# Values of later head groups by seven block products, with their exchange and the reciprocals issued from SP's queue

## The chip, the cores and the metric

The kernel runs on one core of one Trainium2 chip. The metric is the device time of one execution in microseconds (us). TensorE is called PE here and its weight loads PEld; VectorE is DVE, ScalarE is ACT, GpSimd is POOL, and SyncE is SP, which in this kernel does nothing but issue DMAs.

## The reference

The input x has 2048 rows of 256 numbers. It is normalised by row (xn), and the output is x plus two branches of xn, everything in float32:

```python
qkv = jnp.einsum('bsd,ed->bse', x, Wqkv)            # x is xn here; 16 heads of 128
logits = jnp.einsum('bqhd,bkhd->bhqk', q, k) * D ** (-0.5)
w = jax.nn.softmax(logits)
out = jnp.einsum('bhqk,bkhd->bqhd', w, v).reshape(B, S, H * D)
return jnp.einsum('bse,de->bsd', out, Wout)
...
x = x + _L0_attn_ref(xn, Wqkv, Wout) + _L0_ffn_ref(xn, w1, w2, w3)
```

The second branch is a small gated layer with weights rounded to -1, 0 and 1; it is done ahead of the attention loop and is not touched here.

## The kernel before, in words

**Blocks and steps.** The transposed xn lies in SBUF as `xnT` (two slices d of 128 by 2048 columns). The attention is cut into 64 blocks n = 0..63: 16 heads times four query blocks of 512. A block has four steps t = 0..3 of 128 queries. Two heads make a group g (G = 2), so a group has eight blocks, and i = n mod 8 says which of them it is. In the text "step (5,3)" means i = 5, t = 3 in any group.

**What one step of the loop at L965 does.** The scores run ahead by LEAD = 6 steps: step u = 4n + t computes the scores of step v = u + 6, exchanges them, transposes the exponentials of step v - 2, and multiplies block n's transposed exponentials with the values. In the order of the program, each engine taking its own instructions in that order:

- `left` of the step before (L1065): DVE adds up the product of values (`added`, L744, at t = 3 with the multiplication by the spread reciprocals in oT, L754) and reads the second projection product, if there was one.
- POOL's differences (`differences`, L662, line L677): the product with the values is done with seven block products in the place of eight, and the exponentials' side of it needs four differences in each block.
- `scores` (L559): PE makes two halves of 1024 keys in PSUM tiles `s`, of which there are three. DVE takes each half's maximum (L579) and the negated maximum (L582). Then `beside` (L990) makes the step's first projection product on PE into the only buffer of tag `m`, and DVE reads it. ACT makes the exponentials (L589); that frees the `s` tile.
- `inverses` (L615) at t = 2: DVE sums and inverts the row sums, transposes them (L627), and POOL sends them to DRAM (`rd`, L628).
- `transposed` (L652): DVE turns two parts of 128x1024 into a slot of R (L657).
- `weighted` (L706): PE multiplies with the values, 16 pairs of matmuls (8 pairs at t = 3), line L724.
- the step's second projection product, into the same `m` buffer, if the step has two; ACT's `copied` (L733).
- `exchanged` (L595): ten DMAs from SP's queue and two from ACT's, 64 KB each, move 32-row pieces of p into two tiles `part0` and `part1` (two buffers each); ACT copies the other four pieces.
- `between` (L929): POOL's DMAs for the output projection, weight loads and small sums.

At t = 1 `spread` (L630) lets POOL read the reciprocals back, broadcast to all partitions, into oT.

**Projection products.** Steps with t = 2, 3 make the keys and queries of the next head (`fast_product`, L163, `fast_read`, L180): seven 128x128x512 products over two blocks in the place of eight. That form pairs two column blocks of xn and leaves one of its two results with its elements in another order, which the read puts right in its output pattern. Steps with t = 0, 1 of blocks i = 0..3 make the output projection of the group before, also by seven products (`o_product`, L803). Steps with t = 0, 1 of blocks i = 4..7 make the values of the next group (`v_product`, L272, `v_read`, L282): eight products, one in each step, each of 16 PE instructions of 256 columns, and two DVE copies of 128x256. These eight steps have no second product. The table `x_sums` (L155) holds differences of xn's column blocks, made once by POOL.

**The order of the work** is written out by hand (`manual_schedule`); tiles of one tag share buffers, and an instruction waits where a buffer or an operand isn't ready.

Of the kernel before, what the change touches and what calls it, by code (L numbers as in the profile page):

```python
# [9 lines left out]
F32 = mybir.dt.float32  # L10
F32R = mybir.dt.float32r
AF = mybir.ActivationFunctionType
ALU = mybir.AluOpType
# [7 lines left out]
def layernorm_attention_bitffn_kernel(  # L21
# [123 lines left out]
    def weight_sums(h: int):  # L145
# [6 lines left out]
        nc.gpsimd.tensor_tensor(w[:, 3], wk[:, 1], w[:, 1], sub)  # L152
        ws[h] = w

    def x_sums(c: int):  # L155
        t = apool.tile([P, 4, QB], F32, tag=f"t{c}", name=f"t{c}", bufs=1)
        x00, x10 = (xnT[:, d, bass.ts(c, QB)] for d in range(KC))
        x01, x11 = (xnT[:, d, bass.ts(c + 1, QB)] for d in range(KC))
        for i, (a, b) in enumerate(((x01, x00), (x11, t[:, 0]), (x11, x01), (x10, t[:, 1]))):
            nc.gpsimd.tensor_tensor(t[:, i], a, b, ALU.subtract)  # L160
        ts[c] = t

    def fast_product(h: int, b: int, i: int, second: bool):  # L163

        c = b // 2 * 2
        wk, wq = (weights[h // G, i][:, :, bass.ts(h % G, D)] for i in "kq")
        w, t = ws[h], ts[c]
        x00, x10 = (xnT[:, d, bass.ts(c, QB)] for d in range(KC))
        x11 = xnT[:, 1, bass.ts(c + 1, QB)]
        lhs, rhs = {  # L170
            (0, 0): ((wk[:, 0], x00), (w[:, 1], t[:, 1])),
            (0, 1): ((w[:, 2], t[:, 2]), (wq[:, 1], t[:, 3])),
            (1, 0): ((w[:, 0], t[:, 0]), (w[:, 3], x11)),
            (1, 1): ((wk[:, 1], x10),),
        }[b % 2, i][second]
        pm = ps_m.tile([P, QB], F32, tag="m", name=f"pw{h}_{b}_{i}_{int(second)}")
        in_halves(pm, lhs, rhs, True, True)
        return pm

    def fast_read(h: int, b: int, i: int, second: bool, pm):  # L180
        c = b // 2 * 2
        if (b % 2, i) == (0, 0):
            if not second:
                if c == 0:
                    kTs[h] = kvpool.tile([P, S], F32, tag="kT", name=f"kT{h}")
                for j in range(2):
                    qTs[h, c + j] = kvpool.tile(
                        [P, QB], F32, tag="qT", name=f"qT{h}_{c + j}", bufs=NB + 2
                    )
        k0, k1 = (  # L190
            kTs[h].rearrange("p (j k r) -> p k j r", j=P // 32, r=32)[:, j * TB : (j + 1) * TB]
            for j in (c, c + 1)
        )
        q0, q1 = qTs[h, c], qTs[h, c + 1]
        pk = pm.rearrange("p (k j r) -> p k j r", j=P // 32, r=32)
        def q_sum(q, base):
            nc.vector.tensor_tensor(q, pm, base, ALU.add)

        def k_sum(k, base):
            nc.vector.tensor_tensor(k, pk, base, ALU.add)  # L200

        if (b % 2, i) == (0, 0):
            if not second:
                nc.vector.tensor_copy(k0, pk)
            else:
                k_sum(k1, k0)
        elif (b % 2, i) == (0, 1):
            if not second:
                nc.vector.tensor_tensor(
                    q1.rearrange("p (k j r) -> p k j r", j=P // 32, r=32), pk, k1, ALU.add  # L210
                )
            else:
                q_sum(q0, q1)
        elif (b % 2, i) == (1, 0):
            if not second:
                q_sum(q1, q1)
            k_sum(k1, k1)
        else:
            k_sum(k0, k0)
# [38 lines left out]

    wxs = {}

    def sums_of(k, q, name: str):

# [4 lines left out]
        nc.gpsimd.tensor_tensor(w[:, 3], k[:, 1], w[:, 1], ALU.subtract)  # L269
        wxs[name] = w  # L270

    def v_product(g: int, m: int, second: bool):  # L272
        w = weights[g, "v"]
        pm = ps_m.tile([P, 2, G * D], F32, tag="m", name=f"pvw{g}_{m}")
        for j in range(2):
            for d in range(KC):
                in_halves(
                    pm[:, j], xnT[:, d, bass.ts(2 * m + j, P)], w[:, d], d == 0, d == KC - 1
                )
        return pm  # L280

    def v_read(g: int, m: int, second: bool, pm):  # L282
        for j in range(G):
            nc.vector.tensor_copy(
                v_tile(g * G + j)[:, 2 * m : 2 * m + 2], pm[:, :, bass.ts(j, D)]
            )

    ppool = ctx.enter_context(tc.tile_pool(name="ppool", bufs=2))
    front = ExitStack()
# [7 lines left out]
    ods = [  # L297
        [away.tile([P, G, QB], F32, tag=f"od{g}_{c}", name=f"od{g}_{c}") for c in range(NB)]
        for g in range(2)
    ]  # L300
    rds = [away.tile([P, 32], F32, tag=f"rd{i}", name=f"rd{i}") for i in range(2)]

# [312 lines left out]
    def inverses(n: int):  # L615
        if n >= NBK - NB:

            r = small.tile([P, TB], F32, tag="rlast", name=f"rlast{n}")
            nc.vector.tensor_tensor(r, sums[n][:, :, 0], sums[n][:, :, 1], ALU.add)
            nc.vector.reciprocal(r, r)  # L620
            rbs[n] = r
            return
        ri, riT = rinvs[n % 2]
        nc.vector.tensor_reduce(ri[:, :TB], sums[n], AX.X, ALU.add)
        nc.vector.reciprocal(ri[:, :TB], ri[:, :TB])

        nc.vector.transpose(riT, ri)  # L627
        nc.gpsimd.dma_start(rds[n % 2], riT)  # L628

    def spread(n: int):  # L630

        if n < NBK - NB:
            r = rds[n % 2].rearrange("(j c) r -> j (c r)", c=32)[:, : TB * 32]
            nc.gpsimd.dma_start(
                oT.rearrange("p (j x) -> p j x", j=P // 32), r.partition_broadcast(P)
            )
            rbs[n] = oT
# [291 lines left out]
    def between(n: int, t: int):  # L929

        g, i = divmod(n, GB)
        last = NBK - NB

        if t == 1:
            if i == GB - 1 and n < last:
                load_weights(g, "o", nc.gpsimd)
        if t == 2:
            if i == NB - 1 and g + 1 < H // G:
                load_weights(g + 1, "v", nc.gpsimd)
            elif n == last - 1:  # L940
                load_weights(g, "o", nc.gpsimd)
        if g and i < NB:
            o_moved(g - 1, i, t)
        elif n < last:
            if i == GB - 2:
                if t < 3:
                    o_fetched(g, *((0, 0, 0), (1, 0, 1), (1, 1, 2))[t])
                else:
                    o_difference(1, 1, 0)
                    o_difference(2, 2, 1)  # L950
            elif (i, t) == (GB - 1, 2):
                y_moved(0, False)
        if n < last and (i, t) == (GB - 1, 3):
            o_sums(g)
        if n >= last - 1 and t == 2:
            b = n + 1 - last
            nc.gpsimd.dma_start(o3[:, b % 2], ods[(H - 2) // G % 2][b][:, 0])
        if (n, t) in ((last - 2, 3), (last - 1, 0)):
            fetched_back(n + 2 - last)
        if t == 0 and n in (last - 3, last - 2, last, last + 1):  # L960
            x_fetched((last - 3, last - 2, last, last + 1).index(n))

    behind = []
    with tc.manual_schedule():
        for u in range(-LEAD, (NBK - 1) * TB):  # L965
# [13 lines left out]
            if n >= NB and t < 2:  # L979
                i, j = divmod(i, NB)  # L980
                j = 2 * j + t
                if not i:
                    seven, hi = True, (g - 1, j)
                    product, read, twice = o_product, o_read, j % NB != 1
                elif g + 1 < H // G:
                    seven, hi = True, (g + 1, j)
                    product, read, twice = v_product, v_read, False
            pms = []

            def beside():  # L990
# [7 lines left out]

            if behind:
                behind.pop()()  # L1000
            if t == 0 and n >= 0:
                if 0 < n <= NBK - NB:
                    put_away(n - 1)
                differences(n, "T1b")
            elif t == 1 and n >= 0:
                differences(n, "T2h")
                if n >= NB and n % GB < NB and n % 2 == 0 and n < NBK - NB:
                    o_difference(0, 2, 0)
                differences(n, "T3b")
                spread(n)  # L1010
                if blocks[n][1] == 0:
                    v_combined(blocks[n][0], 2)
                    v_combined(blocks[n][0], 3)
                differences(n, "T4")
            elif t == 3 and -1 <= n < NBK - 2:
                differences(n + 1, "T1a")
                if n % 2 and n % GB < NB <= n < NBK - NB - 2:
                    y_moved(n % GB, True)
                differences(n + 1, "T3a")
                if n >= 0 and blocks[n + 1][1] == 0:  # L1020
                    v_combined(blocks[n + 1][0], 0)
                    v_combined(blocks[n + 1][0], 1)
# [118 lines left out]
```

## Time and profile before

| what | us |
| --- | --- |
| median of three runs (lowest, highest) | 2160.19 (2158.59, 2161.88) |
| the profiled execution's own time | 2159.7 |
| its span in the trace | 2157.9 |
| PE busy | 2143.5 |
| DVE busy | 1756.1 |
| POOL busy | 1579.3 |
| ACT busy | 1375.1 |
| values of later groups on PE (`pvw`, 896 instructions) | 107.6 |
| their copies on DVE (L284, 112 instructions) | 42.0 |
| POOL idle ahead of the reciprocals' DMA (L628) | 154.2 |
| SP's queue waiting for DVE's transposes (L611) | 206.1 |

The profile is one execution. Busy time is the union of an engine's instructions. The granted clock of PE is full in every slice. The timeline merges equal instructions that follow one another into one row (start, length, line, operation, tiles, shape, number); a row's length is to the end of its last instruction, and consecutive PE instructions overlap, so the pace is read from start to start of two rows. In the rows of the DMA view, the last number is the median time from the start of an issue to the landing.

### The profile page before, as it was taken

What the parts mean: (1) busy time and instruction counts of PE and PEld (TensorE: products, weight loads), DVE (VectorE), ACT (ScalarE), POOL (GpSimd) and SP (SyncE); (2) the same over time, 40 slices, a digit from 0 to 9 for tenths busy, and PEclk for the clock granted to TensorE, in tenths of its full rate; (3) what the DMA queues carried; (4) which work ended last, traced back from release to release, by engine and by line L of the source; (5) the groups of instructions that cost most, each with busy time, mean ns of one, the idle gap of its engine ahead of it and who ended that gap; (6) DMA issues with size and microseconds to landing.
All of it is one profiled execution on the core that took longest, in us unless ns stands there. A gap on an engine that the chain in (4) does not pass through costs nothing. (4 is left out here: it accounts for less than half of the span.)

```text
span 2157.9 us, 41390 instructions
## 1 busy us (share of the span) xinstructions
PE 2143.5 (99%) x14018; PEld 1207.6 (56%) x14018; DVE 1756.1 (81%) x2394; ACT 1375.1 (64%) x2414; POOL 1579.3 (73%) x1010
## 2 busy tenths in 40 slices
PE   9999999999999999999999999999999999999999
PEld 6745445445655555555555455655555555555556
DVE  6577887888888887888788888788888888788885
ACT  5587766666666666666666666666666666666773
POOL 0067767987678867887768876788767887788873
PEclk9999999999999999999999999999999999999999
DMA  2055555575556655566555754556555665556663
GB/s 94 39 119 139 132 117 136 148 187 142 121 140 160 166 141 128 136 184 157 123 128 142 189 151 110 140 145 180 149 122 135 157 173 143 127 138 184 174 151 95
DMA packets 182341, 304.34 MB, mean 141 GB/s; under 512 B 55088, under 2 KB 60592, under 8 KB 182128
## 3 DMA queue, kind: packets, MB, share of 16 engines
q1 hardware_dynamic: 127856, 175.21, 31.9%
q0 software_dynamic: 28720, 91.97, 17.5%
q10 hardware_dynamic: 25552, 34.51, 6.2%
q8 instruction: 111, 1.82, 0.4%
q14 instruction: 102, 0.84, 0.1%
HBM read 65.60 MB, written 34.54 MB: 46 GB/s over the span
## 5 line engine op out<-in xcount | busy, mean ns | idle before, releaser
L677 POOL TENSOR_TENSOR R<-R 128x1024 f32<-128x1024 f32 x441 | 1175.5, 2673 | 144.4 <-DVE R L657 84.7
L94 PE MATMUL s<-kT,qT 128*64 128x512 f32 x4000 | 907.4, 592 | 1.0 <-ACT p L589 0.8
L613 ACT COPY part<-p 32x512 f32<-32x512 f32 x1024 | 630.7, 616 | 417.7 <-issue 306.5
L579 DVE TENSOR_REDUCE mx<-s 128x1 f32<-128x1024 f32 x512 | 618.2, 1220 | 230.5 <-PE s L94 216.7
L589 ACT ACTIVATE p<-s,nm 128x1024 f32<-128x1024 f32 x512 | 565.9, 1110 | 207.8 <-PE pw L94 101.6
L657 DVE STREAM_TRANSPOSE R<-part 128x1024 f32<-128x1024 f32 x512 | 605.1, 1220 | 34.1 <-DMA part<-p 24.4
L94 PEld LDWEIGHTS s<-kT,qT 128*64 128x64 f32 x4000 | 331.7, 137 | 476.2 <-issue 431.8
L724 PE MATMUL av<-R,v 128*64 128x256 f32 x3728 | 531.2, 379 | 1.5 <-DVE oU L750 1.3
L724 PE MATMUL av<-R,st 128*64 128x256 f32 x3024 | 457.7, 379 | 2.5 <-ACT oU L742 1.3
L724 PEld LDWEIGHTS av<-R,v 128*64 128x64 f32 x3728 | 357.7, 137 | 109.7 <-issue 43.9
L724 PEld LDWEIGHTS av<-R,st 128*64 128x64 f32 x3024 | 305.5, 137 | 143.0 <-issue 50.6
L628 POOL DMA_DIRECT2D rd<-r x60 | 33.4, 556 | 154.2 <-DVE r L627 153.9
L742 ACT COPY oU<-av 64x256 f32<-64x256 f32 x248 | 90.7, 366 | 84.5 <-PE av L724 77.0
L780 POOL DMA_DIRECT2D od<-oU x60 | 34.0, 567 | 125.0 <-DVE oU L754 125.0
L750 DVE TENSOR_TENSOR oU<-av,oU 64x256 f32<-64x256 f32 x248 | 101.8, 411 | 27.4 <-ACT oU L742 24.7
L94 PE MATMUL pvw<-wv,xnT 128*64 128x256 f32 x896 | 107.6, 379 | 0.0
L94 PEld LDWEIGHTS pvw<-wv,xnT 128*64 128x64 f32 x896 | 74.8, 137 | 45.7 <-issue 24.2
L589 ACT ACTIVATION_READ_ACCUMULATOR p<-s,nm 128x1 f32 x512 | 100.3, 196 | 0.0
L824 DVE TENSOR_TENSOR osums<-pow,osums 128x512 f32<-128x512 f32 x108 | 72.5, 682 | 29.3 <-DMA osums<-yd 18.3
L94 PE MATMUL pw<-t,ws 128*64 128x512 f32 x336 | 88.4, 592 | 0.0
L160 POOL TENSOR_TENSOR t<-xnT 128x512 f32<-128x512 f32 x4 | 5.1, 1271 | 107.1 <-DMA part<-p 107.1
L200 DVE TENSOR_TENSOR kT<-pw,kT 128x512 f32<-128x512 f32 x112 | 76.8, 686 | 1.8
(153 smaller groups left out, 1484.4 us busy)
## 6 DMA issues: line engine op xcount, KB each, us to landing
part<-p SPq DMA_DIRECT2D x2560, 64.0 KB, 2.3
part<-p ACTq DMA_DIRECT2D x512, 64.0 KB, 2.6
o<-od POOLq DMA_DIRECT2D x74, 256.0 KB, 3.9
oT<-rd POOLq DMA_DIRECT2D x60, 256.0 KB, 5.5
od<-oU POOLq DMA_DIRECT2D x60, 256.0 KB, 2.7
osums<-yd POOLq DMA_DIRECT2D x28, 512.0 KB, 4.8
yd<-osums POOLq DMA_DIRECT2D x26, 512.0 KB, 3.5
yd<-yT SPq DMA_DIRECT2D x4, 512.0 KB, 2.6
```

The lines of the kernel that those rows point to most:

```text
L94: nc.tensor.matmul(out[c * HP : (c + 1) * HP], lhs[:, c * HP : (c + 1) * HP], rhs, start=start, stop=stop, skip_group_check=True,)
L200: nc.vector.tensor_tensor(k, pk, base, ALU.add)
L579: nc.vector.tensor_reduce(mx[:, i : i + 1], s, AX.X, ALU.max)
L589: nc.scalar.activation(p, s, AF.Exp, bias=nm, scale=SCALE, accum_out=sums[n][:, t, i : i + 1],)
L613: nc.scalar.copy(*ends(j, j))
L657: nc.vector.transpose(to[:, t % 2, 2 * i : 2 * i + 2], part.rearrange("p g (s c) -> p g s c", s=2),)
L677: nc.gpsimd.tensor_tensor(o, x, y, ALU.subtract)
L724: nc.tensor.matmul(av[i * HP : (i + 1) * HP, half], l[:, kk], moving(s, kk), start=start, stop=(k == units[r] - 1), skip_group_check=True,)
L742: nc.scalar.copy(u[op, oq], av[ap, half])
L750: nc.vector.tensor_tensor(u[p, q], av[p, half], u[p, q], ALU.add)
L780: nc.gpsimd.dma_start(ods[h // G % 2][b][:, h % G], oU)
L824: nc.vector.tensor_tensor(to, pm, y, ALU.add)
```

## The change

1. The values of groups 1 to 7 are made by seven block products for each half of the 2048 rows (`fast_v_product`, `fast_v_read`), with the two heads of the group in the places that queries and keys have in `fast_product`. So a group has 14 products of 512 columns in its eight steps: two in each of six steps and one in two. DVE reads them with eight operations on 128x512 for each half.
2. The result is the transposed one (128 numbers of a head by rows of x), while the product with the exponentials wants rows of x on partitions. For each head and half, `v_sent` moves four pieces of 32 partitions to DRAM (4 KB in each partition, 1 KB at a time), `v_landed` reads the half back with its pieces exchanged (512 KB, into columns of `xnT` that are no longer needed), and DVE transposes 32x32 blocks with two instructions of 128x512 (`v_transposed`). The table `v_steps` names the step in which each is issued, at the step's beginning in the new function `ahead`.
3. To free those columns of `xnT`, the second pair of column blocks is taken in the opposite order (`pair`).
4. The DMA of the reciprocals to DRAM (`sent_away`) moves from POOL's queue at t = 2 to SP's at the beginning of t = 3, and `spread` from POOL's queue at t = 1 to SP's at the beginning of t = 2.
5. POOL makes four sums of the value weights (`v_sums`) once in each group at (3,3).

```diff
+    def pair(c: int):
+        return (c, c + 1) if c == 0 else (c + 1, c)
...
+    def v_sums(g: int):
+        wv = weights[g, "v"]
+        sums_of(wv[:, :, D:], wv[:, :, :D], f"wvs{g}")
...
-    def v_product(g: int, m: int, second: bool):
-        w = weights[g, "v"]
-        pm = ps_m.tile([P, 2, G * D], F32, tag="m", name=f"pvw{g}_{m}")
-        for j in range(2):
-            for d in range(KC):
-                in_halves(
-                    pm[:, j], xnT[:, d, bass.ts(2 * m + j, P)], w[:, d], d == 0, d == KC - 1
-                )
+    def fast_v_product(g: int, m: int, second: bool):
+        half, m = divmod(m, NB)
+        wv, w, t = weights[g, "v"], wxs[f"wvs{g}"], ts[2 * half]
+        c0, c1 = pair(2 * half)
+        x00, x10 = (xnT[:, d, bass.ts(c0, QB)] for d in range(KC))
+        x11 = xnT[:, 1, bass.ts(c1, QB)]
+        lhs, rhs = (
+            ((wv[:, 0, D:], x00), (w[:, 1], t[:, 1])),
+            ((w[:, 2], t[:, 2]), (wv[:, 1, :D], t[:, 3])),
+            ((w[:, 0], t[:, 0]), (w[:, 3], x11)),
+            ((wv[:, 1, D:], x10),),
+        )[m][second]
+        pm = ps_m.tile([P, QB], F32, tag="m", name=f"pvw{g}_{half}_{m}_{int(second)}")
+        in_halves(pm, lhs, rhs, True, True)
         return pm
...
-            nc.vector.tensor_copy(
-                v_tile(g * G + j)[:, 2 * m : 2 * m + 2], pm[:, :, bass.ts(j, D)]
-            )
...
+        if (m, second) == (0, False):
+            nc.vector.tensor_copy(k0, pm)
+            return
+        todo = {
+            (0, True): ((k1, k0),), (1, False): ((q1, k1),), (1, True): ((q0, q1),),
+            (2, False): ((q1, q1), (k1, k1)), (2, True): ((k1, k1),), (3, False): ((k0, k0),),
+        }[m, second]
+        for o, i in todo:
+            nc.vector.tensor_tensor(o, pm, i, ALU.add)
+
+    def v_sent(h: int, half: int):
+
+        v = v_half(h, half).rearrange("p k d -> p (k d)")
+        vd = vds[h % G][half].rearrange("(j r) (q c) -> q r j c", r=32, c=S // 8)
+        for q in range(P // 32):
+            nc.sync.dma_start(vd[q], v[bass.ts(q, 32)].rearrange("r (j c) -> r j c", c=S // 8))
+
+    def v_landed(h: int, half: int):
+        nc.sync.dma_start(landing, vds[h % G][half])
+
+    def v_transposed(h: int, half: int):
+        v = v_half(h, half).rearrange("p k (q r) -> p q k r", r=32)
+        w = landing.rearrange("p (q k r) -> p q k r", q=P // 32, r=32)
+        for u in range(2):
+            nc.vector.transpose(v[:, 2 * u : 2 * u + 2], w[:, 2 * u : 2 * u + 2])
+
+    wxs, landing = {}, xnT[:, 0, QB : 3 * QB]
...
-        nc.gpsimd.dma_start(rds[n % 2], riT)
+
+    def sent_away(n: int):
+        nc.sync.dma_start(rds[n % 2], rinvs[n % 2][1])
...
-            nc.gpsimd.dma_start(
+            nc.sync.dma_start(
                 oT.rearrange("p (j x) -> p j x", j=P // 32), r.partition_broadcast(P)
             )
...
+        if t == 3:
+            if i == NB - 1 and g + 1 < H // G:
+                v_sums(g + 1)
...
+    v_steps = {
+        (5, 1): [(v_sent, 0, 0)], (5, 2): [(v_landed, 0, 0), (v_sent, 1, 0)],
+        (5, 3): [(v_transposed, 0, 0)], (6, 0): [(v_landed, 1, 0)], (6, 1): [(v_transposed, 1, 0)],
+        (7, 1): [(v_sent, 0, 1)], (7, 2): [(v_landed, 0, 1), (v_sent, 1, 1)],
+        (7, 3): [(v_transposed, 0, 1)], (8, 0): [(v_landed, 1, 1)], (8, 1): [(v_transposed, 1, 1)],
+    }
+
+    def ahead(n: int, t: int):
+
+        if t == 3 and n + 1 < NBK - NB:
+            sent_away(n + 1)
+        if t == 2 and n >= 0:
+            spread(n)
+        g, i = divmod(n, GB)
+        for late in range(2):
+            if late < g + 1 < H // G + late:
+                for do, j, half in v_steps.get((i + late * GB, t), ()):
+                    do((g + 1 - late) * G + j, half)
...
-                    product, read, twice = v_product, v_read, False
+                    product, read, twice = fast_v_product, fast_v_read, j % NB != NB - 1
...
             if behind:
                 behind.pop()()
+            if n >= -1:
+                ahead(n, t)
...
-                spread(n)
```

## The prediction

> **What bounds the kernel now.** I read the page's busy table first, then PE's timeline through a group's last value block (i = 7) into the next block, then DVE, ACT and SP over the same stretch, then the DMA table.
>
> ```profile
> PE 2143.5 (99%) x14018; PEld 1207.6 (56%) x14018; DVE 1756.1 (81%) x2394; ACT 1375.1 (64%) x2414; POOL 1579.3 (73%) x1010
> ```
> ```profile
> 612.63 1.93 PE L94 MATMUL pvw<-wv,xnT 128*64 128x256 f32 x16
> 614.36 3.65 PE L724 MATMUL av<-R,v 128*64 128x256 f32 x32
> 617.81 3.63 PE L94 MATMUL s<-kT,qT 128*64 128x512 f32 x16
> ...
> 635.03 3.63 PE L94 MATMUL s<-kT,qT 128*64 128x512 f32 x16
> 638.46 1.06 PE L94 MATMUL pw<-xnT,wk 128*64 128x512 f32 x4
> 639.32 1.93 PE L724 MATMUL av<-R,v 128*64 128x256 f32 x16
> 641.04 3.63 PE L94 MATMUL s<-kT,qT 128*64 128x512 f32 x16
> ```
>
> PE has no idle time in the loop: every row starts where the last one's issue ended. From start to start: scores 3.43 us, a value product 1.73, a product of 512 columns 0.86, the product with the exponentials 3.45 (1.72 at t = 3). So work taken from PE is time won, as long as no other engine makes PE wait. The nearest is DVE:
>
> ```profile
> 633.28 2.37 DVE L657 STREAM_TRANSPOSE R<-part 128x1024 f32<-128x1024 f32 x2
> 635.58 0.82 DVE L750 TENSOR_TENSOR oU<-av,oU 64x256 f32<-64x256 f32 x2
> 636.43 0.69 DVE L200 TENSOR_TENSOR kT<-pw,kT 128x512 f32<-128x512 f32 x1
> 637.04 1.21 DVE L579 TENSOR_REDUCE mx<-s 128x1 f32<-128x1024 f32 x1
> 638.70 1.23 DVE L579 TENSOR_REDUCE mx<-s 128x1 f32<-128x1024 f32 x1 [0.45 <-PE s L94]
> 639.96 0.21 DVE L582 TENSOR_SCALAR nm<-mx 128x1 f32<-128x1 f32 x1
> ```
>
> This is step (7,3), the shortest of a block (6.0 us of PE): DVE goes from transposes to sums to the first maximum without a pause and has only 0.45 us left ahead of the second. SP is nearly as full: ten exchange DMAs a step at 0.63 us from start to start are 6.3 us of a step of 6.0 to 8.6.
>
> ```profile
> part<-p SPq DMA_DIRECT2D x2560, 64.0 KB, 2.3
> o<-od POOLq DMA_DIRECT2D x74, 256.0 KB, 3.9
> oT<-rd POOLq DMA_DIRECT2D x60, 256.0 KB, 5.5
> osums<-yd POOLq DMA_DIRECT2D x28, 512.0 KB, 4.8
> yd<-osums POOLq DMA_DIRECT2D x26, 512.0 KB, 3.5
> yd<-yT SPq DMA_DIRECT2D x4, 512.0 KB, 2.6
> ```
>
> **Part 1, PE's gain.** A group's values cost 8 x 1.73 = 13.8 us now and 14 x 0.86 = 12.0 after (the new products have the form of the 512-column rows). 1.8 us in seven groups is **-12.6 us**.
>
> **Part 2, DVE's added work, covered or not.** Reads: sixteen operations of 0.68 us (row L200) in the place of sixteen copies of 0.42: +4.2 us a group. Transposes: eight of 128x512; from 0.21 us at 32 columns and 1.22 at 1024, I take 0.70, so 1.3 us for a pair. Summing a block's steps with these rows, blocks 5 and 7 reach about 29.2 us of DVE in 31.0 of PE, blocks 4 and 6 27 to 28 in 32.7. It fits, so by busy time alone this costs nothing; POOL's four sums (2.2 us a group) lie in its idle time too. But the transposes stand in DVE's order ahead of the step's maxima, so what counts is when the data lands.
>
> **Part 3, the landing at (5,3) and (7,3).** No row shows this DMA: 512 KB from DRAM issued by SP. Bounds: 2.6 us (the same size written from SP, on a quiet chip) and 4.8 (the same read issued by POOL, beside the exchange). I take 3.9, the write's 2.6 plus the 1.3 by which POOL's read exceeds its write. The first landing of a half is issued right behind the oT broadcast, which moves to SP too; as a read of the same size from the same queue takes 3.9 and the broadcast 5.5, its small pieces hold the DMA engines 1.6 us longer. Issued 0.6 us ahead, I charge 1.1 us: **5.0** for this one (bounds 2.6 and 4.8 + 1.6 = 6.4).
>
> Now the order on SP. The landing follows the ten exchange DMAs of step (5,1). In the trace the matching ones start with ACT's exponential:
>
> ```profile
> 623.04 1.11 ACT L589 ACTIVATE p<-s,nm 128x1024 f32<-128x1024 f32 x1 [1.16 <-issue]
> ```
> ```profile
> 631.62 0.59 SPq L611 DMA_DIRECT2D part<-p  x1
> ```
>
> Those two rows say that SP ends the ten 9.2 us after the exponential of (7,1) began. Call that E. Then oT's issue, 0.6; landing at E + 9.2 + 0.6 + 5.0 = E + 14.8. DVE gets to the transposes when its sums of (7,2) are done: the exponential of (7,2) comes one PE step later, E + 7.7 (0.9 sooner than now, since step (7,1) loses 1.73 and gains 0.86), and the sums end at 637.04, 5.4 after that step's exponential at 631.65: E + 13.1. **DVE waits about 1.7 us.**
>
> What PE feels: the exponential at 640.25 begins 1.8 us after the scores' issue end at 638.46. It moves by the pair of transposes 1.3 and the wait 1.7, less the slack 0.45: to 4.35. PE wants that first `s` buffer for the second half of the next scores, 0.86 + 1.72 + 1.72 = 4.3 us after 638.46, and it is free 1.15 after the exponential begins, so anything past 3.15 stalls PE. **1.2 us of stall** (the wait less 0.5), twice in a group: 14 x 1.2 = **+16.8 us**. Without the wait the transposes alone fit, with 0.5 us to spare.
>
> **Part 4, the landing at (6,0).** SP issues it behind the exchange of the late (5,3), which ends 8.1 us after its exponential (640.25 to 648.39): 4.35 + 8.1 + 3.9 = 16.35 us after the scores of (5,3). DVE, with step (6,0)'s work done, is there at about 14.8. It waits 1.5, turns (1.3), and the maxima, the negation and the first read (2.4 + 0.1 + 0.6) end at 20.7. PE wants the only `m` buffer for its second product at (6,1) about 20.1 after. Before, value steps had no second product, so this wait is new: **0.6 us**, in seven groups **+4 us**. At (8,1) there is no second product, and the `s` buffers are free in time: nothing.
>
> **Part 5, the rest.** POOL loses 60 issues of rd (0.56) and of oT (0.78) and 154 us of waiting, but PE waits 3.3 us for POOL's differences in all: at most 3 us won, which I don't count. On SP blocks 5 and 7 get eleven more issues, 51 x 0.63 = 32 us of 31.0; the exchange falls behind by 1 to 2 us there, and its pieces land 5 to 7 us ahead of their transposes. So nothing, unless the lag passes 5 us. The reciprocals get a step more and are not needed until (n,3)'s end. 7 x 4 MB of added traffic is 9% of 304 MB.
>
> **Sum.** -12.6 + 16.8 + 4 = +8 us. The profiled execution's own time is 2159.7 (2157.9 of span and 1.8 around it), 0.5 below the median of 2160.2, so I predict **2168**.
>
> **The Trainium skill.** The page "DMA: Bandwidth & Descriptors", section "Anatomy of one DMA", gives 2.0 us plus bytes at 436 GB/s, an estimate of 3.2 us for 512 KB; for 64 KB that is 2.15, beside 2.3 measured here. By it alone both landings are nearly in time, and the sum would be about -11 us. The same page, "Queues, rings and completion order", says that an engine takes the descriptors of one issuer's ring in order. That speaks against moving oT to SP just ahead of a landing; with it the sum stays near the one above. No row of this trace shows that order for oT.
>
> **Rivals.** (A) *The landing is quick*: 3.5 us or less, oT not in its way. For: a 512 KB write from SP takes 2.6. Against: every read in the table is slower than its write. The waits then cost 0 to 6 us: 2148 to 2154. It decides where the first landing takes less than about 3.8 us. (B) *Gain and waits cancel*: at 4.3 to 4.9 us for the first, 2156 to 2164. (C) *oT blocks longer, or the exchange delays it too*: first landing at 6.4 and second at 4.8 gives waits of 3.1 and 2.4, stalls of 2.6 x 14 + 1.5 x 7 = 47, less 12.6: 2195. (D) *SP overflows*: if the exchange lags over 5 us in blocks 5 and 7, DVE's R transposes wait; each further us costs 14. Against: SP itself now waits 206 us for DVE, which it could spend on issues. (E) *PE doesn't take the products at 0.86*: excluded by four rows of that form.
>
> **Chances.** The forecast (first landing 4.9 to 6) 0.35, A 0.30, B 0.22, C and D together 0.13. What a measurement can tell from no change is 0.2%, 4.3 us. Faster: A, 0.31 with a little of B; same: most of B, 0.22; slower 0.47. The range reaches down to A's full gain less a little, 2149, and up into C, 2190; cases of both signs hold it, and the forecast's own range is 2163 to 2182.
>
> **What would show it.** After: `pvw` rows of four instructions at 0.86; on DVE, a wait of 1 to 2 us for the DMA that writes xnT at (5,3) and (7,3), and at (6,1); on PE, scores waiting for ACT's exponentials at (6,0) and (8,0), 1 to 1.5 us each. If DVE shows no such wait, A holds. If DVE's R transposes wait for part, it is D. I am wrong altogether if PE's idle time in the loop stays near zero, or sits in steps that I have not named.

## The result

| kernel | median, us (lowest to highest) | span of the profiled execution | PE idle after 200 us | lost to a lower clock from 200 us to the last stall |
| --- | --- | --- | --- | --- |
| before | 2160.19 (2157.74 to 2161.88) | 2157.9 | 4.8 | 0.0 |
| changed | 2339.93 (2334.5 to 2347.56) | 2343.9 | 140.4 | 66.6 |

The changed kernel is slower: the ratio is 1.0839, with a 95% interval of 1.0814 to 1.0864. The forecast of 2168 and its range to 2190 are missed by 172 and 150 us. The last column is worked out from the granted clock: the length of each stretch at less than full clock times the missing share. Windows at the start and the very end, which no stall of the loop brings, are left out.

### The profile page after: what moved, and what is told of

It reads as the page before. It is cut to its first block, busy times and chain, and to the rows that moved or that the text cites. A ratio compares the mean times of both kernels' runs of the same rounds, so it can differ in the third digit from the quotient of the medians.

```text
span 2343.9 us, 40558 instructions
## 1 busy us (share of the span) xinstructions
PE 2192.1 (94%) x13514; PEld 1058.9 (45%) x13514; DVE 1816.6 (78%) x2450; ACT 1375.6 (59%) x2414; POOL 1513.4 (65%) x918
## 5 line engine op out<-in xcount | busy, mean ns | idle before, releaser
L94 PE MATMUL s<-kT,qT 128*64 128x512 f32 x4000 | 948.8, 615 | 102.2 <-ACT p L645 102.2
L715 DVE STREAM_TRANSPOSE R<-part 128x1024 f32<-128x1024 f32 x512 | 605.2, 1220 | 40.9 <-DMA part<-p 39.6
L94 PEld LDWEIGHTS s<-kT,qT 128*64 128x64 f32 x4000 | 300.1, 141 | 661.7 <-issue 497.5
L782 PEld LDWEIGHTS av<-R,v 128*64 128x64 f32 x3728 | 330.3, 138 | 153.4 <-issue 63.9
L782 PEld LDWEIGHTS av<-R,st 128*64 128x64 f32 x3024 | 287.4, 137 | 196.3 <-issue 74.0
L335 DVE STREAM_TRANSPOSE v<-xnT 128x512 f32<-128x512 f32 x56 | 36.5, 690 | 181.3 <-DMA xnT<-vd 91.5
L849 POOL TENSOR_TENSOR o<-o 128x512 f32<-128x512 f32 x56 | 73.1, 1306 | 1.3
L319 DVE TENSOR_TENSOR v<-pvw,v 128x512 f32<-128x512 f32 x98 | 65.1, 676 | 5.2 <-PE pvw L94 4.9
```

The costliest lines, as they stand in the source:

```text
L94: nc.tensor.matmul(out[c * HP : (c + 1) * HP], lhs[:, c * HP : (c + 1) * HP], rhs, start=start, stop=stop, skip_group_check=True,)
L715: nc.vector.transpose(to[:, t % 2, 2 * i : 2 * i + 2], part.rearrange("p g (s c) -> p g s c", s=2),)
L782: nc.tensor.matmul(av[i * HP : (i + 1) * HP, half], l[:, kk], moving(s, kk), start=start, stop=(k == units[r] - 1), skip_group_check=True,)
L849: nc.gpsimd.tensor_tensor(o3[:, slot], o3[:, x], o3[:, y], ALU.subtract)
```

## The profile after

The page of the changed kernel: the span, the busy table, a group of PE (busy time, mean ns | idle time ahead of it and what ended it), the group of the new transposes, and DMAs that the change adds or moves.

```profile
span 2343.9 us, 40558 instructions
...
PE 2192.1 (94%) x13514; PEld 1058.9 (45%) x13514; DVE 1816.6 (78%) x2450; ACT 1375.6 (59%) x2414; POOL 1513.4 (65%) x918
...
L94 PE MATMUL s<-kT,qT 128*64 128x512 f32 x4000 | 948.8, 615 | 102.2 <-ACT p L645 102.2
...
L335 DVE STREAM_TRANSPOSE v<-xnT 128x512 f32<-128x512 f32 x56 | 36.5, 690 | 181.3 <-DMA xnT<-vd 91.5
...
oT<-rd SPq DMA_DIRECT2D x60, 256.0 KB, 5.6
vd<-v SPq DMA_DIRECT2D x112, 128.0 KB, 2.2
xnT<-vd SPq DMA_DIRECT2D x28, 512.0 KB, 6.5
```

PE has 504 matmuls fewer, and yet its busy time has grown by 49 us and it stands idle. DVE spends 36.5 us on the new transposes and 181.3 us in front of them. So the time is lost where the prediction looked for it, but in another size. The list of waits (us in total, times, longest) has the same places, and that of SP's queue one more, its sends of the values:

```profile
DVE R L715 <- DMA part<-p: 39.6, 30, 3.7
...
PE pvw L94 <- DVE v L319: 31.7, 7, 5.9
```
```profile
SPq L326 <- DMA part<-p: 79.8, 17, 7.9
```

One pass through steps (7,2) to (8,0), on SP, DVE and PE in the timeline (start, length):

```profile
952.84 7.39 SPq L667 DMA_DIRECT2D part<-p  x10
960.39 1.61 SPq L692 DMA_DIRECT2D oT<-rd  x1
962.10 0.45 SPq L329 DMA_DIRECT2D xnT<-vd  x1
967.31 2.29 SPq L326 DMA_DIRECT2D vd<-v  x4
969.71 8.17 SPq L667 DMA_DIRECT2D part<-p  x10
```
```profile
962.58 0.69 DVE L205 TENSOR_TENSOR kT<-pw,kT 128x512 f32<-128x512 f32 x1
968.70 1.30 DVE L335 STREAM_TRANSPOSE v<-xnT 128x512 f32<-128x512 f32 x2 [5.43 <-issue]
...
992.38 1.30 DVE L335 STREAM_TRANSPOSE v<-xnT 128x512 f32<-128x512 f32 x2 [9.00 <-DMA xnT<-vd]
```
```profile
967.22 1.88 PE L94 MATMUL s<-kT,qT 128*64 128x512 f32 x8
973.84 3.63 PE L94 MATMUL s<-kT,qT 128*64 128x512 f32 x8 [4.74 <-ACT p L645]
```

The landing is issued at 962.10, behind oT, and lands at 968.62. DVE, ready at 963.27, waits 5.43 us; the scores' second half then waits 4.74 us for an `s` buffer. The eight matmuls that follow take 3.41 us from start to start of the next row, twice what eight took before (3.43 us for sixteen). The view by windows says why; its columns are the window, its length, PE's busy time, the granted clock, the DMA share and GB/s:

```profile
969.10:973.84 4.74, 0.00 (x1) 1.00 0.59 137
973.84:977.25 3.41, 3.41 (x9) 0.51 0.41 96
977.25:981.61 4.36, 4.36 (x38) 0.99 0.49 139
```

After the stall PE is granted half its clock for a window. In the loop after the first 200 us the trace has 27 such windows of 3.41 or 6.83 us, 133 us together; the kernel before has none there. They are why PE's busy time grew.

Where the time went, by steps: for each step the time from its first scores matmul to the next step's is added up over the groups, and that of the kernel before is taken off (us; the other kernels are the experiments below).

| kernel | (5,1), (7,1) | (6,0) | (6,1), (6,2) | (8,0) | (8,2) | (6,3), (8,1), (8,3) | others | all |
| --- | --- | --- | --- | --- | --- | --- | --- | --- |
| changed | -12.2 | +48.5 | +46.8 | +54.0 | +39.8 | -0.3 | +6.7 | +183.3 |
| reciprocals on POOL | -12.2 | +23.1 | +49.3 | +37.8 | +43.2 | -0.3 | -1.6 | +139.3 |
| transposes five times, no exchange | -12.2 | +45.2 | +16.1 | +41.1 | +9.0 | -0.3 | +15.8 | +114.7 |
| exchange without transposes | -12.2 | +2.1 | +28.7 | +7.1 | 0.0 | +32.5 | +39.5 | +97.7 |
| the same, reciprocals on POOL | -12.2 | -0.1 | +1.3 | +3.8 | 0.0 | +36.5 | +4.4 | +33.7 |
| early landings, POOL sends and lands | -12.2 | -0.1 | -0.1 | 0.0 | 0.0 | +4.4 | -1.6 | -9.6 |

Three things are to be seen. The gain is there in every kernel, in (5,1) and (7,1), the two steps that make one product of 0.86 us in the place of one of 1.73. In the changed kernel the loss sits in four places of seven groups, each of which has one stall; one of the 28 stalls, at (8,2), has no window behind it. And where nothing waits for a landing, the loss is in other steps.

## The experiments

The theories were these. **Landing**: the transposes stand on DVE ahead of the maxima and wait for a landing that comes late, and PE pays for DVE's wait (Parts 3 and 4). **SP**: the values' and the reciprocals' transfers ahead of the exponentials make the exponentials late (rival D). The expectations also name a DVE theory (DVE's added work is too much by itself), and call the SP theory, from run 5 on, that of the queues. Ratios are to the kernel before, run on the same chip, with 95% intervals. Runs 5 to 8 were made on one chip and the others on another; the medians of the kernel before are 1 to 3 us apart, and differences between runs of the two chips carry that much.

**1. The products alone.** The table of the exchange is empty; the reciprocals stay on SP.

```diff
-    v_steps = {
...
+    v_steps = {}
```

> The change without the exchange of the values: seven block products and their reads stay, nothing is sent to DRAM, read back or transposed, so the values of groups 1 to 7 stay in the wrong layout. Landing theory (DVE stands at its transposes until the DMA from DRAM lands, PE stalls behind it 28 times for some 4.9 us and runs at half clock for a while after each): all of the loss goes and PE's gain of 12.6 us shows, 2146 to 2150. DVE theory (the added reads are too much for DVE in blocks 5 and 7): part of the loss stays, above 2200. SP theory (the queue is too full with 140 more issues and the reciprocals): most of the loss goes, but the reciprocals on SP keep some of it, 2165 to 2200.

Measured 2157.66 us, ratio 0.9996 (0.9985 to 1.0007). The steps (5,1) and (7,1) gain 12.2 us; the time doesn't, as PE stands idle 13.0 us, mostly in (2,0) to (4,2), in front of DVE's sums. None of the three expected ranges holds it. Run 15 shows that this comes from the reciprocals.

**2. The transposes without transfers.** The entries of `v_sent` and `v_landed` are taken out of the table.

> As the one before, with DVE's 56 transposes back in their places, but of whatever lies in xnT: no DMA to DRAM or from it, so the transposes wait for nothing. The values of groups 1 to 7 are wrong. Landing theory: the work alone fits, within 4 us of the kernel without them, 2146 to 2152. DVE theory: the transposes' place ahead of the maxima is enough to stall PE, at least 14 times 2 us with half clock after, 2200 or more. SP theory: as the kernel without them.

Measured 2158.97 us, ratio 1.0001 (0.9991 to 1.001), as the run before it. DVE's added work costs nothing by itself; Part 2 stands.

**3. The exchange without the transposes.** The entries of `v_transposed` are taken out.

> The change without DVE's 56 transposes: the pieces are sent to DRAM and read back by SP as in the change, but nobody waits for the landing. The values of groups 1 to 7 are wrong. Landing theory: SP's lag and the traffic cost little, as nobody stands behind them: 2146 to 2160. SP theory: the loss is all there, above 2250, since the exchange of the exponentials comes late by as much as in the change.

Measured 2263.23 us, ratio 1.0488 (1.0459 to 1.0518). Nothing waits for a landing here, and 105 us are lost against run 1. DVE's transposes of the exponentials wait instead, and SP for its earlier transfers:

```profile
DVE R L715 <- DMA part<-p: 173.8, 102, 6.2
```
```profile
SPq L667 <- DMA part<-p: 181.7, 126, 4.6
```

The first was 24.4 us before. So the landing theory alone falls: rival D is real. In the changed kernel it hardly shows (39.6 us); my reading, which no run tests, is that DVE is held at the values' transposes first and SP catches up meanwhile.

**4. The kernel before with the reciprocals on SP.**

```diff
-        nc.gpsimd.dma_start(rds[n % 2], riT)
...
+            if t == 3 and -1 <= n and n + 1 < NBK - NB:
+                sent_away(n + 1)
+            if t == 2 and n >= 0:
+                spread(n)
```

> The kernel before with the reciprocals' two DMAs moved to SP's queue as in the change, and nothing else. Landing theory: not on any path that PE waits for, 2156 to 2164, no difference. SP theory: 120 more issues, one of them of many small pieces in the ring of the exchange, cost something by themselves, 2170 to 2220.

Measured 2171.2 us, ratio 1.0046 (1.003 to 1.0061): 12.3 us for moving two transfers a block, without any values.

**5. The changed kernel with the reciprocals on POOL.** `rd` and oT go back to POOL's queue, to their old places.

> The changed kernel with the two transfers of the reciprocals issued from POOL again, in their old places; the values' products, exchange and transposes as changed. Landing theory (the transposes stand on DVE ahead of their landings, which take 7.1 us in the median behind oT and 5.15 us without it): only the first landing gets shorter, by about 2 us, 14 of 28 stalls shrink by 2 us, and the time is about 2300 us, with DVE still waiting 4 to 7 us at every transpose. Theory of the queues (oT's pieces of 512 bytes hold SP's and ACT's transfers for about 4 us, and the transfers of the exponentials behind them come late): most of the stalls fall under the 2.5 us from which the clock was halved, and the time is between 2160 and 2210 us, with few halved windows. If the time stays within 10 us of 2340 us, the reciprocals have no part in the loss.

Measured 2297.79 us, ratio 1.0652 (1.0629 to 1.0674). DVE's mean wait for the first landing falls from 5.82 to 3.65 us, that for the second only from 7.13 to 6.78. This is what the landing theory expected; 42 of the 180 us belong to the reciprocals.

**6. Run 3 with the reciprocals on POOL.**

> The run with the exchange of the values but without its transposes (2263.2 us), now with the reciprocals issued from POOL; the transposes are left out, so v isn't the reference's. Nothing on an engine waits here for the landings of the values. Theory of the queues with oT as the cause: what is left of the loss goes with oT, 2150 to 2165 us. Theory of the queues with the values' own ten issues per head as the cause (4 to 6 issues of 0.63 us and a landing ahead of the ten of the exponentials): still 2210 to 2250 us, with DVE waiting for part at the same steps as before. Landing theory has nothing to say here, beyond what the transposes would add.

Measured 2189.4 us, ratio 1.0131 (1.0104 to 1.0157), between the two expectations: the reciprocals made 74 us of run 3's loss, the values' own transfers on SP the other 43 (against run 15). DVE still waits 126.9 us for exponentials.

**7. Early landings.** The reciprocals on POOL; the sends of a half's first head and both landings are issued at the end of the step before, just ahead of `exchanged` (the expectations call a step a part). The transposes stay where they were.

```diff
+    v_early = {
+        (5, 0): [(v_sent, 0, 0)], (5, 1): [(v_landed, 0, 0)], (5, 3): [(v_landed, 1, 0)],
+        (7, 0): [(v_sent, 0, 1)], (7, 1): [(v_landed, 0, 1)], (7, 3): [(v_landed, 1, 1)],
+    }
...
+            if n >= 0:
+                v_issued(v_early, n, t)
             if more:
                 exchanged(v)
```

> Reciprocals on POOL, and the landings issued a step part earlier than they were, ahead of that part's ten transfers of the exponentials, so that a landing has a whole part (about 15 us) before its transposes. Landing theory: no transpose waits, no stall is left, and the time is 2146 to 2156 us, which beats the kernel before by 0.2 to 0.6%. Theory of the queues with the values' own issues as the cause: the exponentials' transfers still come behind them, DVE waits for part at (5,1), (5,2), (7,1), (7,2) and one part later, and the time is 2180 to 2260 us, about that of the exchange without transposes and with the reciprocals on POOL.

Measured 2181.42 us, ratio 1.0107 (1.0089 to 1.0125): 116 us less than run 5. No transpose waits for a landing, and (6,0) and (8,0) lose nothing to speak of. What is left is SP's part, as the second theory had it, at the low end.

**8. Early landings, the reciprocals still on SP.**

> As the run with early landings and the reciprocals on POOL, but the reciprocals stay on SP. It differs from that run by oT and rd on SP's queue alone. Landing theory: 2155 to 2170 us (the 10 to 13 us that the reciprocals on SP cost without any exchange of values, and nothing more). Theory of the queues with oT as the cause: 2230 to 2270 us, as the exchange without transposes (2263.2 us), since the transposes wait for nothing and the exponentials are late behind oT as there.

Measured 2231.2 us, ratio 1.0331 (1.031 to 1.0352). This is the low end of the second theory: oT and rd on SP cost 50 us beside the values' transfers, where they cost 12 alone.

**9 and 10. DVE held, with no transfer.** Run 2 with its transposes done five and three times over:

```diff
-        for u in range(2):
+        for u in [0, 1] * 5:
```

> The run with the transposes without any exchange (2158.97 us), its four transposes per group done five times over, so that DVE is held 5.3 to 5.5 us longer at each of the four places, with no transfer added (v isn't exchanged, so it isn't the reference's). In the changed kernel DVE waited 5.8 and 7.1 us at these places. Theory that the held DVE is what costs (PE stalls in the two parts that follow, and a stall from about 2.3 us on is followed by a window of 3.41 or 6.83 us at half clock): 28 stalls of 3 to 4 us, 25 or so halved windows, idle of PE 90 to 115 us, clock loss 40 to 60 us, 2290 to 2330 us. Rival (the loss is made by the transfers that run at that time, and the wait is only where it shows): 2159 to 2180 us.

> The same with the transposes done three times over: DVE held 2.7 us longer at each place. If a held DVE costs PE what goes past the scores that PE has ahead (2 to 2.5 us, as the stall in the changed kernel was about 2 us shorter than the wait), the stalls are under 1 us, no window is halved, and the time is 2160 to 2180 us: less than a sixth of what the five-fold transposes cost. If each held us cost PE a us, 28 x 2.7 = 76 us, 2235 us.

Measured 2274.26 us for five, ratio 1.0528 (1.051 to 1.0545), and 2197.55 us for three, 1.0183 (1.0166 to 1.0199). Ten transposes take 6.04 us and two 1.28, so DVE is held 4.8 and 2.4 us longer, less than I had put down. PE's first stall after it, with five and with three:

```profile
870.06 3.68 PE L94 MATMUL s<-kT,qT 128*64 128x512 f32 x8 [3.95 <-ACT p L645]
```
```profile
912.28 1.94 PE L94 MATMUL s<-kT,qT 128*64 128x512 f32 x8 [1.59 <-ACT p L645]
```

This first stall is the hold less 0.8 us in both, and it was the wait less 0.7 in the changed kernel. The long stalls of run 9 sit in the changed kernel's own steps, with no transfer of values in the trace, so a held DVE is enough to make them. The eight matmuls behind the longer stall take twice their time, those behind the shorter one don't:

```profile
870.06:873.74 3.68, 3.68 (x10) 0.50 0.38 87
```
```profile
912.28:916.00 3.72, 3.72 (x24) 1.00 0.37 87
```

Five-fold holds cost 115 us over run 2, three-fold ones 39: half of the hold costs a third. The 115 are less than the 131 or more that were expected, with 15 windows where 25 were. My 2160 to 2180 for three was too low, since I took PE's cover for 2 us and more where it is 0.8.

**11 and 12. The values' transfers on POOL's queue.** Run 7 with the sends issued by POOL (11), and the landings too (12):

```diff
-            nc.sync.dma_start(vd[q], v[bass.ts(q, 32)].rearrange("r (j c) -> r j c", c=S // 8))
+            nc.gpsimd.dma_start(vd[q], v[bass.ts(q, 32)].rearrange("r (j c) -> r j c", c=S // 8))
...
-        nc.sync.dma_start(landing, vds[h % G][half])
+        nc.gpsimd.dma_start(landing, vds[h % G][half])
```

> The early landings with the reciprocals on POOL (2181.42 us), and the four sends of each head's half now issued from POOL too, so that SP issues only one transfer (the landing) per half ahead of the exponentials. Theory that SP's own issues for the values make the exponentials late: (0,3), (0,1), (6,3) lose nothing any more, 2146 to 2160 us, the first version that beats the kernel before. Rival (the bytes or the pieces of the values hold the exponentials, on whichever queue): 2170 to 2185 us, as without the move. Rival (POOL stands at a send until DVE's read, and its sums come late): over 2185 us.

> As the run before it, but the landing of each half is issued from POOL as well: SP and ACT carry the exponentials alone, as in the kernel before. Theory of SP's issues: 2146 to 2156 us, a little below the run with the landings on SP. If a landing (512 KB) on SP is what holds the exponentials and not the sends, this run gains against that one by 10 us or more. If POOL, standing at a landing until the sends have landed, becomes late with R's sums, it is slower than that one.

Measured 2152.9 us, ratio 0.9968 (0.9955 to 0.9981), and 2150.82 us, ratio 0.9962 (0.9948 to 0.9977). Both beat the kernel before. Moving four sends per head's half away from SP is worth 28.5 us between the medians, 30 against each run's own kernel before; moving the landings too makes no difference that can be told. In run 12 the bytes of the values are the same, and the waits for the exponentials are back to what they were:

```profile
DVE R L713 <- DMA part<-p: 17.0, 14, 2.7
...
POOL vd L326 <- DVE v L319: 12.3, 14, 0.9
```

POOL does stand 12.3 us at the sends. That isn't quite free: DVE waits 12.4 us for POOL's differences (8.1 before), each time at (8,2), just ahead of the 4.4 us that (8,3) loses in the table.

**13 and 14. oT in larger pieces.** The same bytes from the same buffer, in 128 pieces of 2 KB, in run 4's kernel (13) and in the changed one (14):

```diff
-            r = rds[n % 2].rearrange("(j c) r -> j (c r)", c=32)[:, : TB * 32]
+            r = rds[n % 2].rearrange("(j c) r -> j (c r)", j=1)[:, :QB]
```

> The kernel before with the reciprocals issued from SP (2171.2 us against 2158.85), with oT read as 128 pieces of 2 KB from the same buffer instead of 512 pieces of 512 bytes: the same bytes, the same issue, another order of values (so not the reference's). Theory that the pieces hold the rings: oT lands in under 4 us instead of 5.6, and the time goes back to 2158 to 2163 us. Rival (two more issues ahead of ten, and the wait of the issue for the reciprocals): 2168 to 2173 us, as with small pieces.

> The changed kernel with oT in 128 pieces of 2 KB instead of 512 of 512 bytes (not the reference's values). Theory that the pieces hold the rings: the landing of the values behind oT comes about 2 us earlier, the second stalls stay, and the time is near that of the changed kernel with the reciprocals on POOL (2297.8 us), 2290 to 2310 us. Rival (the place of the issues): 2330 to 2345 us, as changed.

Measured 2158.8 us, ratio 1.0002 (0.9992 to 1.0011), and 2313.63 us, ratio 1.0715 (1.0693 to 1.0736), 4 us above the first theory's range. The 12.3 us of run 4 are gone, with the issues in the same place. SP's queue in the page's third part and oT in the DMA view, small pieces first:

```profile
q1 hardware_dynamic: 168176, 191.93, 36.3%
...
oT<-rd SPq DMA_DIRECT2D x60, 256.0 KB, 5.7
```
```profile
q1 hardware_dynamic: 145136, 191.93, 35.9%
...
oT<-rd SPq DMA_DIRECT2D x60, 256.0 KB, 3.7
```

23,040 packets fewer (60 times 512 less 128) with the same megabytes, and 2.0 us less to land. In the changed kernel the larger pieces win back 26 of the 42 us that the reciprocals on SP cost there; the other 16 are left, which I put down to the place of the issues without a test.

What these two runs don't tell apart is how the pieces cost time. They can stand in the way of the transfers behind them, or SP can wait with its next issues until oT has landed. SP's queue in run 4 and in run 13:

```profile
SPq L611 <- DMA oT<-rd: 30.1, 31, 2.1
```
```profile
SPq L611 <- DMA oT<-rd: 1.4, 4, 0.7
```

The exchange needs nothing from oT, yet SP waits for it 31 times with small pieces and 4 times with large ones. The end of the next section says what these waits have in common.

**15. The products alone, reciprocals on POOL.**

> The values' products by seven alone, without their exchange and transposes (so v isn't the reference's), and with the reciprocals on POOL in their old places. The prediction's first part alone: 14 steps of 0.87 us less, 2145 to 2149 us; if the reads and sums on DVE and POOL cost anything, more than that: up to 2157 us.

Measured 2146.28 us, ratio 0.994 (0.9924 to 0.9957), 12.1 us below the kernel before, in the middle of what was expected.

From run to run the loss builds up so: products alone 2146.3; with the exchange issued by SP 2189.4 (run 6); with the transposes waiting for it 2297.8 (run 5); with the reciprocals on SP 2339.9 (changed). The steps are 43, 108 and 42 us. They depend on their order, as the 50 and 74 us for the reciprocals in runs 8 and 3 show.

## Why the prediction was wrong

The likeliest direction, the places of three of the four stalls and the engine that causes them were right. The size was not: 8 us forecast, 180 measured.

- **Part 1** holds. -12.6 us were forecast; 12.2 show in the steps, and 12.1 in run 15.
- **Part 2** holds: run 2.
- **Part 3, the landing at (5,3) and (7,3), failed in two terms.** Counted from the exponential E of (7,1), medians of 14: DVE was to be free at E + 13.1 and is at E + 13.2. The ten transfers were to end at E + 9.2 and end at E + 10.6, with four sends ahead of them that the sum had left out (2.06 us of SP in the pass shown); oT's issue takes 0.6 as forecast in the median (1.61 in that pass), and the landing is issued at E + 11.4. It was to take 5.0 us and takes 7.1, beyond the upper bound of 6.4. In run 5, without oT ahead, it takes 4.75: so the transfer itself was put 0.85 too low, and oT's hold, charged at 1.1, is 2.35. It lands at E + 18.6, not E + 14.8, and the wait is 5.5, not 1.7.
- **Part 4, the landing at (6,0), failed mainly in SP's order.** The landing takes 5.15 us (median) in the place of 3.9. But the ten transfers ahead of it end 12.7 us after their exponential, not 8.1: the second head's sends in (7,2) are queued between the landing and the ten, and SP stood at them from 962.55 to 967.31. Some 4.6 us from this and 1.25 from the landing turn a wait of 1.5 into 7.1 in the mean. "At (8,1) nothing" was wrong too: the same wait there delays the next exponential, and (8,2) loses 39.8 us.
- **The step from wait to stall** was good for the first landing: the wait less 0.5, where 0.7 is measured (0.8 in runs 9 and 10). At (6,1) it was the wait less 0.9, where 2.4 is measured (6.9 us of wait, 4.5 of stall in the mean), so there PE was better covered than forecast.
- **No term stood for the clock.** Each us of stall was charged as one us. Half the clock in a window after each long stall took 66.6 us more. So 135.6 of idle time and 66.6 of clock, less 12.6, come to 190 beside the 186 by which the span grew.
- **Part 5 failed.** "So nothing" for SP rested on a count of issues, 32 us of 31, and a lag of 1 to 2 us. The count leaves out that SP's issues wait; with the values' transfers on SP the kernel is 43 us slower (run 6 against run 15). "The reciprocals cost nothing" was wrong by 12 us alone (run 4) and 42 here. Rival D had 0.13 together with C, and its argument, that SP has 206 us of waiting to spend, wasn't enough: 59 of them lie in blocks 5 and 7, by my sum over the steps of the trace, and in run 6 SP waits only 9 there. It did spend that time, and the exponentials were late all the same (126.9 us of DVE's waiting for them in run 6).
- **The bounds** were too low for both landings. Behind oT the median of 7.1 is above the upper bound of 6.4, and the second landing's 5.15 is above the 4.8 that rival C took. So even C, worked out from these bounds, came to 2195.

What stays open is why SP stood at the sends. They need nothing from the transfers of the exponentials, yet the waits name these. By the semaphore events of the trace the DMAs of SP and ACT share eight completion semaphores in turn, and the one of the send at 967.31 was last used by a transfer of ACT's that had landed at 967.29. All 17 of the waits that make up the 79.8 us end in this way, when a transfer of ACT's lands that had the send's semaphore before it. In the changed kernel 21 of SP's exchange transfers, with 30.0 us of waiting together, take over oT's semaphore and start when oT has landed. POOL's DMAs have eight semaphores of their own in the trace, so runs 11 and 12 take the sends out of the turn as well as off SP. This is read, not tested: how much of the loss on SP comes from these waits, and how much from the issues and pieces themselves, stays open.

## What to carry to other kernels

A wait put on an in-order engine ahead of work that feeds the busiest one costs that one the wait less its cover; give a landing a whole step more before the instruction that needs it, and price a stall of more than 3 us at the stall plus half a clock window (1.7 or 3.4 us here). A DMA queue that issues a transfer every step is not free for others because its issues fit by count: ask what each added transfer waits for, and how many pieces it has. Two moves that each looked free, of the sends and of the reciprocals onto SP, cost more together than alone; the same transfers on POOL's queue cost at most some 5 us.

## What the runs showed of the hardware

- **The clock after a stall.** In the changed kernel and runs 3, 5, 6, 8, 9, 10 and 14 together, PE's stalls of 3.2 us or more were followed by a window at half clock in 84 of 87 cases, those of 2.0 to 3.2 us in 26 of 47, those of 0.8 to 2.0 us in 1 of 95. The windows last 3.41 us or twice that and begin 2 to 5.5 us after the stall's start. The Trainium skill, "TensorE: Matmul & The Clock Gate", section "Part 1: The HAM clock gate", has a free-running activity window of 3413 ns, after which an idle PE gets half the clock; the length agrees. Its advice, in "Why this matters for your kernels", to avoid gaps over some 3 us is a little lax here, as half of the stalls between 2.0 and 3.2 us had their window.
- **Small pieces and two queues.** oT's 512 packets of 512 bytes ran from 962.67 to 966.66 in the pass shown. The landing behind it on SP's queue began at 965.22, and the two transfers that ACT had issued at 961.88 and 962.45, on a queue of their own, at 965.05; they took 5.4 and 6.4 us, where the median for ACT's is 2.2. The same page as in the prediction, "DMA: Bandwidth & Descriptors", "Queues, rings and completion order", has an engine take one ring's descriptors in order. The landing's start 2.55 us behind oT's fits that; runs 13 and 14 show that larger pieces land sooner, and not the order itself. The page's fixed cost and rate, which it gives for DMAs issued by GpSimd, made an estimate of 3.2 us for the landing; the medians here are 7.1 behind oT and 5.15 for the second one.
